# A graph network's attention and three graph convolutions: one-hots made by ScalarE, sort and exponentials through PSUM, and gathered rows moved inside SBUF

## The chip, the cores and the metric

The kernel runs on one core of a Trainium2 chip. A core has five engines that each run their own list of instructions in order: TensorE (PE in the profile, its weight loads PEld), VectorE (DVE), ScalarE (ACT), GpSimd (POOL) and SyncE (SP), which here issues most DMAs. Sixteen DMA engines move data between DRAM (HBM), and the on-chip memory SBUF, which has 128 partitions; TensorE writes its results into PSUM, a second memory of 128 partitions in banks. Engines wait for each other through semaphores. The metric is the device time of one execution in microseconds (us); lower is better. The kernel before takes 6156.63 us, the median of three runs (6151.24 to 6157.75).

## What is computed

A graph of 12500 nodes with 128 features and 200000 edges, sorted by their destination. In short:

```python
h = relu(layernorm(x))
q, k, v = h @ Wq.T, h @ Wk.T, h @ Wv.T                 # 8 heads of 16
scores = einsum(q[dst], k[src]) / 4 + edge_attr @ We.T  # per edge and head
ex = exp(scores - segment_max(scores, dst)[dst])
x = x + segment_sum(v[src] * ex, dst) / segment_sum(ex, dst)
h = relu(layernorm(x))
# three times, with self loops and norm = deg**-.5 at both ends:
#   h = segment_sum((h @ W)[src] * norm, dst) + b ; (relu) ; batch_norm over the nodes
x = x + h
```

All is float32.

## The kernel before

The destination nodes are cut into 106 tiles of 118 (`TN`); a tile's edges lie in a window of 2048 consecutive edges (16 on each of 128 partitions). The program is written in a framework that takes the order of instructions on each engine from priorities and its own plan of the work, and adds all semaphores; each engine then runs its list in that order, and a buffer of a pool is reused when its last reader is done.

**Prologue.** Layer norm, q and the pairs k, v are computed and written to DRAM.

**Attention** (`fast`, from line 885). For each tile GpSimd issues 16 indirect gathers (`gather`, line 148) of 128 rows of k and v into one of three `kv` buffers. VectorE makes `oht` (line 1013), which tells for each edge which of the 128 nodes is its destination, from the edges' node numbers `dw_b`. TensorE multiplies it with q (line 1019), VectorE multiplies the result with k (line 1020) and sums within heads (line 1023). After the edges' bias, scans along the edges give each destination's maximum (lines 1051 to 1075). ScalarE takes the exponential (line 1081), VectorE multiplies it with v (`vals`, line 1082) and makes the second one-hot `oh`, of 16 x 118 columns (line 677), and TensorE sums per node (line 1089).

**Sort.** Between the tiles' instructions, from tile 24 on, `place_edges` prepares the convolutions: a bitonic sort of each tile's edges by source, with all tiles side by side on 106 partitions. Each of its steps is two VectorE instructions of 1024 elements (`swap`, lines 701 and 702). Further steps rank the edges and place each into a slot: for each tile and each of 98 blocks of 128 source nodes there are 13 slots (`SB`), and edges beyond go to an overflow list of at most 768 (`OV`). `go_on` takes the next steps of this at four places of each tile.

**Convolutions** (`conv_slots`). h, scaled, lies in SBUF as `hs` (98 blocks) and in DRAM as `t_d`. The tiles are taken in 12 blocks of nine (9 x 13 = 117 rows). `take` goes through the 98 blocks of sources in seven groups of 14: VectorE turns slot numbers into one-hots `go` (line 1221), TensorE picks the rows (line 1224), ScalarE copies them to `stage` (line 1226), and SP stores `stage` to a table `m` in DRAM (line 1228). `reduce` works one block behind: for each tile six indirect gathers fetch the overflow rows, SP reads the tile's slots from `m` as `mr`, 128 partitions with 10 rows each (line 1245), VectorE makes the one-hot of 16 x 118 from `nums`, a copy of 0 to 117 in PSUM (line 1249), and TensorE sums 10 + 6 products (lines 1253 and 1255) and the tile's own rows (`tg`, line 1159). `finish` does this for three tiles at a time (`GN`), scales, and `use1` to `use3` apply weights, bias and relu. The results h of a convolution stay in SBUF in `big`; only the second half of the first one's 256 features goes to DRAM. When all tiles are done, the batch norm's factors go into the next weights, and `transform` multiplies h by these and writes the next `hs` and `t_d`. If a tile had more overflow than fits, another path (`conv_rows`) would gather each edge's row.

## Time and profile before

| | us |
|---|---|
| median of three runs | 6156.63 |
| the profiled execution | 6154.56 |
| its span | 6152.8 |
| prologue | 0 to 148 |
| attention with the sort | 148 to 2963 |
| the three convolutions | 3008 to 4028, 4091 to 5071, 5113 to 6093 |
| the two transforms, the end | 4034 to 4085, 5076 to 5106, 6097 to 6153 |
| busy: PE, DVE, ACT, POOL | 4406.0, 3396.2, 1011.7, 4084.2 |

The page of a profile gives, for one execution, the busy time of each engine, the span in 40 slices with each engine's busy share in tenths, the DMA engines' share and the TensorE clock that was granted, and then groups of instructions: line, engine, operation, output<-inputs, count, busy time, mean ns of one, and the idle time of the engine just before them with what ended it. Other views show single lines, the instructions in order of time, busy times in chosen stretches, and who waited for whom.

### The profile page before, as it was taken

The numbers are of one execution on the slowest core, as the hardware profiler recorded it, in microseconds if no ns is written. First come the engines' busy times: TensorE is split into PE (matmuls) and PEld (weight loads), VectorE is DVE, ScalarE is ACT, GpSimd is POOL, SyncE is SP. The second block draws the span as 40 slices with busy tenths as digits, with TensorE's granted clock in tenths as the row PEclk, the third lists the DMA queues.
The fourth block names the chain that finished last, engine by engine and source line by source line (L and its number), as shares of the span: only waits on it lengthen the run. The fifth ranks groups of instructions, "written<-read, shape, count | busy, mean of one in ns | idle before, by whom it ended". The sixth has DMA issues, their size and how long they took to land. (4 is left out here: it accounts for less than half of the span.)

```text
span 6152.8 us, 80384 instructions
## 1 busy us (share of the span) xinstructions
PE 4406.0 (72%) x28564; PEld 4115.5 (67%) x28564; DVE 3396.2 (55%) x5972; ACT 1011.7 (16%) x2374; POOL 4084.2 (66%) x3617
## 2 busy tenths in 40 slices
PE   6676666666666665767487787877787787778777
PEld 2666655555566665666377777777777776777777
DVE  7566688887876677655243343353343344434344
ACT  3111111110111111111112122111121211112120
POOL 0777788888888888777266566636666664666663
PEclk9677766666676776767788888898888888888888
DMA  6555544433444444454588888878888887888888
GB/s 188 152 143 138 137 112 106 113 103 109 105 128 120 122 112 112 131 132 114 150 214 216 218 216 218 213 209 217 219 216 221 213 211 204 219 219 219 221 215 209
DMA packets 607714, 1051.07 MB, mean 171 GB/s; under 512 B 191227, under 2 KB 418491, under 8 KB 607201
## 3 DMA queue, kind: packets, MB, share of 16 engines
q1 hardware_dynamic: 464311, 695.85, 41.5%
q0 software_dynamic: 142608, 348.39, 23.9%
q8 instruction: 232, 3.80, 0.3%
q14 instruction: 175, 1.43, 0.1%
q10 hardware_dynamic: 388, 1.60, 0.1%
HBM read 773.19 MB, written 272.26 MB: 170 GB/s over the span
## 5 line engine op out<-in xcount | busy, mean ns | idle before, releaser
L148 POOL DMA_INDIRECT rows<-t_d,srcO x1908 | 1827.6, 958 | 1329.2 <-issue 560.2
L148 POOL DMA_INDIRECT kv<-kv_d,srcA x1696 | 2252.3, 1328 | 536.7 <-issue 484.3
L1249 DVE TENSOR_TENSOR oh<-nums,dlS 128x1888 f32<-128x1888 f32 x318 | 674.3, 2121 | 1527.2 <-PE zp L1255 1517.9
L1253 PE MATMUL zp<-oh,mr 128*128 128x118 f32 x6360 | 966.6, 319 | 567.5 <-DMA mr<-m 440.4
L1253 PEld LDWEIGHTS zp<-oh,mr 128*128 128x128 f32 x6360 | 925.5, 233 | 586.4 <-DMA mr<-m 348.7
L1019 PE MATMUL qe<-qt,oht 128*128 128x128 f32 x3392 | 841.4, 415 | 247.3 <-DVE kv L1020 110.7
L1224 PE MATMUL gp<-hs,go 128*117 128x128 f32 x7056 | 891.8, 281 | 125.8 <-DVE go L1221 69.8
L1019 PEld LDWEIGHTS qe<-qt,oht 128*128 128x128 f32 x3392 | 767.1, 310 | 289.7 <-issue 166.8
L1224 PEld LDWEIGHTS gp<-hs,go 128*117 128x117 f32 x7056 | 831.9, 184 | 165.1 <-issue 117.1
L1226 ACT COPY stage<-gp 117x512 f32<-117x512 f32 x1008 | 521.8, 532 | 1375.0 <-PE gp L1224 936.8
L1020 DVE TENSOR_TENSOR kv<-qe,kv 128x512 f32<-128x512 f32 x424 | 289.4, 685 | 678.8 <-DMA kv<-kv_d,srcA 536.8
L1089 PE MATMUL acc<-vals,oh 128*118 128x137 f32 x3392 | 539.8, 329 | 150.5 <-DVE vals L1082 150.0
L1089 PEld LDWEIGHTS acc<-vals,oh 128*118 128x118 f32 x3392 | 522.1, 225 | 171.6 <-DVE vals L1082 171.3
L1221 DVE TENSOR_SCALAR go<-gi,iota_q 128x468 f32<-128x468 uint8 x1008 | 427.8, 456 | 224.5 <-DMA gi<-gi_d 111.8
L1255 PE MATMUL zp<-oh,rows 128*128 128x118 f32 x3816 | 513.2, 288 | 0.2 <-DMA rows<-t_d,srcO 0.2
L1255 PEld LDWEIGHTS zp<-oh,rows 128*128 128x128 f32 x3816 | 492.2, 206 | 0.4 <-DMA rows<-t_d,srcO 0.4
L1058 PE MATMUL ends<-ident,mg 128*8 128x128 f32 x212 | 53.0, 343 | 344.4 <-DVE mg L1053 305.6
L1082 DVE TENSOR_TENSOR vals<-kv,vals 128x2048 f32<-128x2048 f32 x106 | 242.3, 2286 | 27.2 <-ACT vals L1081 26.8
L1058 PEld LDWEIGHTS ends<-ident,mg 128*8 128x8 f32 x212 | 11.7, 96 | 366.1 <-DVE mg L1053 298.8
L1023 DVE TENSOR_REDUCE sc<-kv 128x128 f32<-128x2048 f32 x106 | 240.8, 2272 | 0.0
L677 DVE TENSOR_TENSOR oh<-iota_f,dlA 128x1888 f32<-128x1888 f32 x106 | 224.0, 2113 | 5.0 <-PE acc L1089 5.0
L1036 PE MATMUL sm<-wbd,et 128*128 128x32 f32 x848 | 167.8, 351 | 45.0 <-DVE mg L1075 37.7
(242 smaller groups left out, 3648.1 us busy)
## 6 DMA issues: line engine op xcount, KB each, us to landing
m<-stage SPq DMA_DIRECT2D x252, 784.0 KB
mr<-m SPq DMA_DIRECT2D x318, 560.0 KB
dw_b<-dlb_d SPq DMA_DIRECT2D x106, 512.0 KB
gi<-gi_d SPq DMA_DIRECT2D x252, 204.8 KB
rows<-t_d,srcO POOLq DMA_INDIRECT x1908
kv<-kv_d,srcA POOLq DMA_INDIRECT x1696
ebx<-in_edge_attr_dram SPq DMA_DIRECT2D x106, 256.0 KB
mr<-m SPq DMA_DIRECT2D x318, 75.0 KB
```

The lines of the kernel that those rows point to most:

```text
L148: nc.gpsimd.indirect_dma_start(out=o, out_offset=None, in_=table[:, :], in_offset=bass.IndirectOffsetOnAxis(ap=idx, axis=0))
L1019: nc.tensor.matmul(qe[:, k, :], ohv[:, :, j + k], qt, start=True, stop=True)
L1020: nc.vector.tensor_tensor(qk[:, j:j + 4, :], qe, qk[:, j:j + 4, :], op=ALU.mult)
L1023: nc.vector.tensor_reduce(sc.rearrange("p h j -> p j h"), qk.rearrange("p j (h c) -> p j h c", h=H), AX.X, ALU.add)
L1082: nc.vector.tensor_tensor(vh[:, :, :, :C], kv[:, :, D:].rearrange("p j (h c) -> p j h c", h=H), vh[:, :, :, C:].to_broadcast([P, JJ, H, C] ...
L1089: nc.tensor.matmul(acc, oh[:, j, :], va[:, j, :], start=(j == 0), stop=(j == JJ - 1))
L1221: nc.vector.tensor_scalar(go[:, :n], gv[:, a:a + n], iota_q, None, op0=ALU.is_equal)
L1224: nc.tensor.matmul(gp[:, i, :], go[:, i].rearrange("p t k -> p (t k)"), hs[:, g * SG + a + i, :], start=True, stop=True)
L1226: nc.scalar.copy(stage[:, a:a + n, :], gp[:, :n, :])
L1249: nc.vector.tensor_tensor(oh, nums.unsqueeze(1).to_broadcast(sh), dlS[:, t, :].unsqueeze(2).to_broadcast(sh), op=ALU.is_equal)
L1253: nc.tensor.matmul(zp[:, i, :], mr[:q, j, :], oh[:q, j, :], start=False, stop=False)
L1255: nc.tensor.matmul(zp[:, i, :], rows[:, j, :], oh[:, RC + j, :], start=False, stop=(j == JO - 1))
```

## The change

In the attention `oht` and `oh` are now made by ScalarE: the absolute value of a difference, then relu(1 - that), which is 1 where the two numbers are equal and 0 elsewhere. The exponentials go to PSUM (`ex`), from which VectorE takes them for `vals` and ScalarE copies them into `vals`' last columns. In the sort each step is cut into two halves, and of each half ScalarE first copies the upper operand to PSUM (`hc`); since there are twice as many pieces, `go_on` takes two at each place. PSUM tiles `nb` and `sm` share buffers, and `acc` has one buffer instead of two.

In the convolutions there are 16 slots instead of 13, an overflow of 512 instead of 768, so four gathers for a tile instead of six, and blocks of eight tiles (14 of them; 8 x 16 = 128 rows). `m` in DRAM is gone: SP moves `stage` from SBUF to SBUF, into `mr`, which holds all eight tiles. Partition q x 16 + s of `mr` holds slot s of a group of 7 (first part) or 6 (second part) sources; the first part has 8 such groups, the second 7. Each transfer fills the 16 partitions of one group from the 128 partitions of `stage`. The sums run in two parts as well: `add_first` adds 7 products for a tile into PSUM while the second part is being taken, `add_rest` adds the own rows, 6 products and the 4 of the overflow while the next block's first part is being taken. Four tiles share a PSUM tile, which a matmul with zeros opens. `big` is gone: all of h goes to DRAM (`h_d`) and is read back by `transform` and by the last stage.

```diff
 WE = 2048
 MG = 4
-SB = 13
-OV = 768
+SB = 16
+OV = 512
 JO = OV // P
 TB = P // SB
-GN = 3
-SG = 14
+CA, CB = 7, 6
 NOT = 1 << 23
...
-    assert TB % GN == 0
-    RC = -(-SL // P)
-    LP, LR = divmod(SL, RC)
-    assert NS % SG == 0 and 112 < LP < P and LR and RC * P <= WE and NS * P * P < LATE and TN < P
+    assert TB * SB == P and TB % NG == 0 and SL <= WE and NS * P * P < LATE and TN < P
+
+    NA = TB * CA
+    NQ = (NS - NA) // CB
+    assert NA + NQ * CB == NS and NQ <= TB
+    parts = [(0, CA, TB), (NA, CB, NQ)]
+    RC = CA + CB
+
+    batches = [[(0, q, 2) for q in range(0, TB, 2)], [(1, q, min(2, NQ - q)) for q in range(0, NQ, 2)]]
+    MB = 2 * CA
     NBK = -(-NTT // TB)
 
...
+        def batch(b, part, q, m):
+            s0, n, _ = parts[part]
+            s0, n = s0 + q * n, n * m
+            return s0, n, gi_d[b, TB * SB * s0:TB * SB * (s0 + n)].rearrange("(t k) -> t k", t=TB)
...
             def swap(lo, hi, lo2, hi2):
-                nc.vector.tensor_tensor(lo2, lo, hi, op=ALU.min)
-                nc.vector.tensor_tensor(hi2, lo, hi, op=ALU.max)
+                n, d = lo.shape[1:]
+                for k in range(2):
+                    cut = (slice(None), slice(k * n // 2, (k + 1) * n // 2)) if n > 1 else (
+                        slice(None), slice(None), slice(k * d // 2, (k + 1) * d // 2))
+                    hc = ps.tile([P, WE // 4], FP, name="hc")[:NTT].rearrange(
+                        "t (n d) -> t n d", n=max(1, n // 2))
+                    nc.scalar.copy(hc, hi[cut])
+                    yield
+                    nc.vector.tensor_tensor(lo2[cut], lo[cut], hc, op=ALU.min)
+                    nc.vector.tensor_tensor(hi2[cut], lo[cut], hc, op=ALU.max)
...
+            niota = once.tile([P, 1], FP, name="niota")
+            nc.vector.tensor_scalar(niota, iota_q, -1.0, None, op0=ALU.mult)
+
+            def where_zero(x):
+
+                nc.scalar.activation(x, x, AF.Relu, bias=ones[:, 0:1], scale=-1.0)
+
...
                     oht = wk.tile([P, WE], FP, name="oht")
-                    nc.vector.tensor_scalar(oht, dw_b, iota_q, None, op0=ALU.is_equal)
+                    nc.scalar.activation(oht, dw_b, AF.Abs, bias=niota[:, 0:1])
+                    where_zero(oht)
...
-                    nc.scalar.activation(vh[:, :, :, C], mx.rearrange("p h j -> p j h"), AF.Exp)
+                    nc.scalar.activation(ex, mx.rearrange("p h j -> p j h"), AF.Exp)
                     nc.vector.tensor_tensor(vh[:, :, :, :C], kv[:, :, D:].rearrange("p j (h c) -> p j h c", h=H),
-                                            vh[:, :, :, C:].to_broadcast([P, JJ, H, C]), op=ALU.mult)
-                    go_on(1)
+                                            ex.unsqueeze(3).to_broadcast([P, JJ, H, C]), op=ALU.mult)
+                    nc.scalar.copy(vh[:, :, :, C], ex)
+                    go_on(2)
                     oh = wk.tile([P, JJ, TN], FP, name="oh")
-                    one_hot(oh, dlA[:, t, :])
-                    acc = ps2.tile([TN, H * (C + 1) + 1], FP, name="acc")
+                    for j in range(JJ):
+                        nc.scalar.activation(oh[:, j, :], iota_f[:, :TN], AF.Abs, bias=dlA[:, t, j:j + 1], scale=-1.0)
+                    where_zero(oh)
+                    acc = ps1.tile([TN, H * (C + 1) + 1], FP, name="acc")
                     for j in range(JJ):
                         nc.tensor.matmul(acc, oh[:, j, :], va[:, j, :], start=(j == 0), stop=(j == JJ - 1))
                     nc.scalar.copy(att[:, i, :], acc)
...
+                def pool(name, bufs, **kw):
+                    return s.enter_context(tc.tile_pool(name=name, bufs=bufs, **kw))
+
+                gy, gx, sg, mt, ga, ohs, wk = (pool(n, b) for n, b in (("gy", 2), ("gx", 3), ("sg", 2), ("mt", 2),
+                                                                         ("ga", 6), ("ohs", 2), ("wk", 2)))
+                pn, pg, pz, ph = (pool(n, b, space=PSUM) for n, b in (("pn", 1), ("pg", 2), ("pz", 3), ("ph", 2)))
+                nums = pn.tile([P, TN], FP, name="nums")
                 nc.vector.tensor_copy(nums, iota_f[:, :TN])
-                blocks = s.enter_context(tc.tile_pool(name="blocks", bufs=3, space=DRAM))
-                gy = s.enter_context(tc.tile_pool(name="gy", bufs=3))
-                gx = s.enter_context(tc.tile_pool(name="gx", bufs=3))
-                sg = s.enter_context(tc.tile_pool(name="sg", bufs=2))
-                mt = s.enter_context(tc.tile_pool(name="mt", bufs=3))
...
+                def ones_at(dl):
+                    oh = ohs.tile([P, CB + JO, TN], FP, name="oh")
+                    sh = [P, dl.shape[1], TN]
+                    nc.vector.tensor_tensor(oh[:, :sh[1]], nums.unsqueeze(1).to_broadcast(sh),
+                                            dl.unsqueeze(2).to_broadcast(sh), op=ALU.is_equal)
+                    return oh
+
+                def take(b, part, mr):
+                    n = parts[part][1]
+                    for _, q, m in batches[part]:
+                        s0, w, slots = batch(b, part, q, m)
+                        gi = gy.tile([P, P * MB], U8, name="gi")
+                        nc.sync.dma_start(gi[:, :P * w], slots.rearrange("t k -> (t k)").unsqueeze(0)
+                                          .to_broadcast([P, P * w]))
+                        gv = gi[:, :P * w].rearrange("p (t s k) -> p s k t", t=TB, k=SB)
+                        stage = sg.tile([P, MB, D], FP, name="stage")
+                        for a, c in groups(w, 4):
+                            go = gx.tile([P, 4, SB, TB], FP, name="go")
+                            nc.vector.tensor_scalar(go[:, :c], gv[:, a:a + c], iota_q, None, op0=ALU.is_equal)
+                            gp = pg.tile([P, 4, D], FP, name="gp")
+                            for i in range(c):
+                                nc.tensor.matmul(gp[:, i, :], go[:, i].rearrange("p k t -> p (k t)"),
+                                                 hs[:, s0 + a + i, :], start=True, stop=True)
+                            nc.scalar.copy(stage[:, a:a + c, :], gp[:, :c, :])
+                        for i in range(m):
+                            nc.sync.dma_start(mr[(q + i) * SB:(q + i + 1) * SB, :, :n, :],
+                                              stage[:, i * n:(i + 1) * n, :])
                         yield
 
-                def reduce(b, m):
-                    for t0 in range(b * TB, min(NTT, (b + 1) * TB), GN):
-                        n = min(GN, NTT - t0)
-                        zp = ps.tile([P, GN, TN], FP, name="zp")
-
-                        def add(i):
-                            t = t0 + i
+                zps = {}
...
+                def add_first(b, mr):
+                    for t in range(b * TB, min(NTT, (b + 1) * TB)):
+                        if t % NG == 0:
+                            zps[t // NG] = pz.tile([P, NG, TN], FP, name="zp")
+                            nc.tensor.matmul(zps[t // NG].rearrange("p a b -> p (a b)"), zero[:, :P], zero,
+                                             start=True, stop=False)
+                        zp = zps[t // NG][:, t % NG, :]
+                        oh = ones_at(dlS[:, t, :CA])
+                        for j in range(CA):
+                            nc.tensor.matmul(zp, mr[:, t % TB, j, :], oh[:, j, :], start=False, stop=False)
+                        yield
+
+                def add_rest(b, mr):
+                    K = NQ * SB
+                    for t0 in range(b * TB, min(NTT, (b + 1) * TB), NG):
+                        n = min(NG, NTT - t0)
+                        tg = own_rows(wk, table, t0, n)
+                        for t in range(t0, t0 + n):
+                            zp = zps[t // NG][:, t % NG, :]
                             rows = ga.tile([P, JO, D], FP, name="rows")
                             for j in range(JO):
                                 gather(rows[:, j, :], table, srcO[:, t, j:j + 1])
+                            oh = ones_at(dlS[:, t, CA:])
+                            nc.tensor.matmul(zp, tg[:, t - t0, :], ident[:TN, :TN], start=False, stop=False)
+                            for j in range(CB):
+                                nc.tensor.matmul(zp, mr[:K, t % TB, j, :], oh[:K, j, :], start=False, stop=False)
                             for j in range(JO):
+                                nc.tensor.matmul(zp, rows[:, j, :], oh[:, CB + j, :], start=False,
+                                                 stop=(j == JO - 1 and t == t0 + n - 1))
+                            yield
+                        finish(wk, t0, n, zps.pop(t0 // NG), use, ph)
+
+                tiles = iter(())
+                for b in range(NBK):
+                    for part in range(2):
+                        mr = mt.tile([P, TB, CA, D], FP, name="mr")
                         done = 0
+                        for g, _ in enumerate(take(b, part, mr)):
+                            while done < g * TB // (len(batches[part]) - 1):
                                 next(tiles, None)
                                 done += 1
+                        for _ in tiles:
+                            pass
+                        tiles = add_rest(b, mr) if part else add_first(b, mr)
+                for _ in tiles:
+                    pass
+
...
+        def result(wk, t0, n, z, func, bias, st, to):
+
+            h = wk.tile([P, NG * TN], FP, name="h")
+            nc.scalar.activation(h[:, :n * TN], z, func, bias=bias)
+            nc.vector.bn_stats(st[:, t0 // NG, :], h[:, :min(n * TN, N - t0 * TN)])
+            nc.sync.dma_start(to[:, t0 * TN:(t0 + n) * TN], h[:, :n * TN])
...
+        def load_h(sr, h, s0, n):
+            hb = sr.tile([P, NG * P], FP, name="hb")
+            nc.sync.dma_start(hb[:, :n * P], h[:, s0 * P:(s0 + n) * P])
+            return hb
+
+        def transform(sr, ps, wa, row, table):
 
             for s0, n in groups(NS, NG):
-                parts = [big[:, s0 * P:(s0 + n) * P]]
-                for h in more:
-                    hb = sr.tile([P, NG * P], FP, name="hb")
-                    nc.sync.dma_start(hb[:, :n * P], h[:, s0 * P:(s0 + n) * P])
-                    parts.append(hb)
+                fs = [load_h(sr, h, s0, n) for h in h_d[:len(wa)]]
                 tp = ps.tile([P, NG, D], FP, name="tp")
                 for i in range(n):
...
```

`go_on(1)` becomes `go_on(2)` in all four places; `big` is replaced by `hb` in the last stage; `own_rows` is the part of `finish` that loads `tg`.

## The prediction

> **What bounds the kernel now.** I read the page first (shares, slices, costliest groups), then the answer for the gathers' line, the timeline of two attention tiles, the busy times by stage, and TensorE's waits in the second convolution.
>
> ```profile
> span 6152.8 us, 80384 instructions
> ...
> POOL 0777788888888888777266566636666664666663
> PEclk9677766666676776767788888898888888888888
> DMA  6555544433444444454588888878888887888888
> ...
> L148 POOL DMA_INDIRECT rows<-t_d,srcO x1908 | 1827.6, 958 | 1329.2 <-issue 560.2
> L148 POOL DMA_INDIRECT kv<-kv_d,srcA x1696 | 2252.3, 1328 | 536.7 <-issue 484.3
> ```
>
> Two halves with two limits. To 2963 us the attention runs: GpSimd at 0.7 to 0.8, DMA half idle. After it DMA is at 0.8 and GpSimd lower. The gathers of both halves, by line (minimum, median, maximum ns):
>
> ```profile
> L148 POOL DMA_INDIRECT rows<-t_d,srcO x1908: 938/944/1194, 2973.1 to 6088.0; - x191
> L148 POOL DMA_INDIRECT kv<-kv_d,srcA x1696: 941/947/6207, 148.2 to 2930.9; - x189
> L1020 DVE TENSOR_TENSOR kv<-qe,kv x424: 625/691/693, 177.5 to 2934.1; 128x512 f32<-128x512 f32 x142
> ```
>
> Both kinds have the same median, but attention's stretch to 6207. Where, the timeline shows (start, duration, engine):
>
> ```profile
> 1498.80 2.11 DVE L677 TENSOR_TENSOR oh<-iota_f,dlA 128x1888 f32<-128x1888 f32 x1
> 1498.87 2.86 POOL L148 DMA_INDIRECT kv<-kv_d,srcA  x1 [0.30 <-DVE A L702]
> ...
> 1502.03 0.95 POOL L148 DMA_INDIRECT kv<-kv_d,srcA  x1 [0.30 <-issue]
> 1502.47 0.33 SPq L1007 DMA_DIRECT2D qt<-q_d  x1
> 1502.48 0.69 DVE L1020 TENSOR_TENSOR kv<-qe,kv 128x512 f32<-128x512 f32 x1 [0.43 <-PE qe L1019]
> ```
>
> A gather that starts under the one-hot takes 2.86 us and ends with it; one beside L1020, which reads PSUM, takes 0.95. The engine is otherwise back to back: 1676 of 1696 gathers follow the previous one by 0.30 us. So attention lasts as long as GpSimd's chain: 1696 x (0.947 + 0.30) = 2115 us unhindered, plus 2252.3 - 1696 x 0.947 = 646 us of stretching.
>
> ```profile
> 3008.00:4028.00 1020.00, 805.78 (x6096) 776.03 (x6096) 402.19 (x543) 211.04 (x406) 586.68 (x614) 0.88 0.81 214
> 4091.00:5071.00 980.00, 770.49 (x5950) 752.13 (x5951) 383.60 (x510) 191.30 (x371) 608.34 (x635) 0.88 0.84 216
> 5113.00:6093.00 980.00, 768.22 (x5952) 750.21 (x5952) 382.77 (x510) 191.25 (x371) 609.17 (x635) 0.88 0.85 217
> ```
>
> The three convolutions (busy PE, weight loads, DVE, ACT, POOL, clock, DMA share, GB/s): DMA 0.81 to 0.85 with PE at 0.79. What PE waits for in the second:
>
> ```profile
> PE zp L1253 <- DMA mr<-m: 157.4, 31, 8.5
> PE zp L1253 <- issue: 29.9, 6, 5.1
> PE gp L1224 <- DVE go L1221: 12.1, 11, 8.5
> ```
>
> So the rows' way through DRAM sets the pace.
>
> [...]
>
> **Part 1, attention.** *Removed stretching.* I laid each long gather against the VectorE instructions running beside it: L1082 (vals) answers for some 183 us, L677 (oh) 158, L1013 (oht) 93, L701 and L702 (sort) 134; together 568 of 646. All four go or get a PSUM input. 78 remain (the ranking steps after the sort).
>
> *Added.* ScalarE per tile: [...] 10.5 us. Before, ScalarE had (85.5 + 195.8 + 86.5)/106 = 3.5. Now 14; during the sort 264 copies of 0.5 in 39 tiles bring 17. GpSimd's pace is 16 x 1.25 = 20 us, so ScalarE fits below it. Table loads keep their number (59 in either order).
>
> VectorE: in the first 602 us it was busy 371 for about 24 tiles, 15 a tile; less 2.1 + 1.3, and less some 1.5 for the loads of edges later, leaves 10.2. Sort halves cost 0.61 each (L1020's spacing) x 528 = 322 over tiles 24 to 63 in the built order: 8.3 a tile, total 19. The ranking, 157 us, now falls into nine tiles instead of 28: 17 a tile, total 27. There VectorE, not GpSimd, is the bound.
>
> *Sum.* 24 tiles x 20.8 = 499; 39 x 22.5 = 878 (VectorE 19, waiting for ScalarE's copies in order; with no waits 20.5, with many 27); 9 x 31 = 279; 34 x 20.4 = 694; tail 35: 2385 against 2815 (148 to 2963). **Gain 430**, from 250 to 550. The chain of one tile after its last gather (about 16 us from the groups' means) has 40 us in three kv buffers. The 112 and more small writes of slot tables (12 before) cost SP 0.35 each, 40 us in all, beside a queue with room; nothing, at most 40.
>
> **Part 2, the convolutions.** *TensorE.* Spacing in the trace is 0.121 for each half of a 128-column matmul, 0.1115 for 118. Slots 13 to 16 make blocks of 8 tiles, not 9: 14 blocks, 98 x 14 x 2 x 0.121 = 332 (285 before). Per tile 7 + 6 + 4 + 1 matmuls instead of 10 + 6 + 1: 106 x 18 x 2 x 0.1115 = 426 (402). So 758 against 687: 71 dearer, 56 a block.
>
> *DMA removed:* write and read of m, 70 + 69 MB per convolution (191 + 252 us of engine time by the packets), a third of the rows' gathers (168 to 112). GpSimd loses 636 gathers and was not the bound. *Added:* 14 x 98 x 64 KB = 90 MB from SBUF to SBUF. Each transfer, 459 or 393 KB, lands on 16 partitions[...]. [...] about 16 (90 MB at 26 GB/s an engine, the trace's best 7168-byte packet at 272 ns). [...]
>
> *A block.* Other traffic per engine: slots' tables 6.4, dinv 3.4, own rows 3.5, gathers 8: 21 us. [...] I take 8 as not hidden, bounds 2 and 21. In the built order each part's first sum stands only 0.2 to 5.3 us of PE work behind its last source, with two stage buffers; PE thus waits for a landing while at most two batches are in flight: 7 us of idle queue a block, bounds 3 and 9. 59 + 8 + 7 = **74 a block** (68 to 80). 14 x 74 + 20 for filling = 1056 against 980: +76, thrice **+228**. The first convolution's 40 extra stay.
>
> *h through DRAM.* The two transforms (51 and 30 us) and the end (56) each read 6.4 MB more at about 237 GB/s, 27 each; some is loaded ahead: **+65** (45 to 80). Stores of h run in the block's spare engine time; the group of four and its zero matmul (27 x 0.2) count nothing.
>
> *Total.* -430 + 228 + 65 = -137: span 6016. The profiled execution took 6154.56, its span 6152.8, the median is 6156.63: forecast 6015 to 6020 for the median, I give 6015.
>
> **Rivals.** [...] (two transfers to neighbouring partitions overlap). Then PE bounds: 56 + 4 of boundary waits, 14 x 60 + 20 = 860, -120 each: -430 - 360 + 65, 5430. [...]
>
> *Slower: [...]* They stand on SP's queue with the tables and own rows[...]: 59 + 16 + 9 = 84 a block, 1196, +216 each, total +283: 6435. It decides from 77.3 us a block on, where three times +122 eats 430 - 65. Near my 74, hence its weight.
>
> *ScalarE becomes attention's bound:* exp and the sort's copies queue behind 6 us of one-hots, tiles stay at 26 us, 50 gained: 6395. Against: 14 to 17 of 20 us.
>
> That the change falls back to the slower row-wise path needs over 512 overflow edges in a tile; the inputs have at most 476.
>
> **Chances.** A run tells about 0.2% from none. Likeliest case 0.42 (68 to 80 a block: 5764 to 6268; faster 0.35, same 0.03, slower 0.04)[...], ScalarE 0.10 (0.03 still faster). Faster 0.62, same 0.03, slower 0.35. The range 5420 to 6450 leaves out the ends of the outer cases.
>
> **What would show it.** kv gathers with a mean near 1.0 us and the last one near 2350 (right), a pace of 26 us a tile with ScalarE full (wrong). In the convolutions: packets of 3584 bytes above 400 ns and PE waiting for mr<-stage[...], or near 150 ns and PE above 0.9 busy[...]. VectorE's instructions of 1.2 us on L723 would show the sort's halves dearer.

## The result, and the profile after

The changed kernel takes 6999.28 us (median of 4 runs, 6996.75 to 7007.39), the kernel before beside it 6157.19: **13.7% slower**, a ratio of 1.1367 with a 95% interval of 1.1347 to 1.1387. The forecast was 6015 us, 5420 to 6450.

The page of the kernel after, in the same parts as shown of before:

```profile
POOL 1767677766866762233323212333323123333230
PEclk8777777777677777888888868787878778878787
DMA  6666555544455647888888858888888888888888
...
L153 POOL DMA_INDIRECT rows<-t_d,srcO x1272 | 1236.6, 972 | 3009.8 <-PE zp L1302 1332.1
L153 POOL DMA_INDIRECT kv<-kv_d,srcA x1696 | 1713.2, 1010 | 747.7 <-issue 466.2
```

In 40 slices of 175 us, attention now ends in the sixteenth, and DMA is at 0.8 to the end. GpSimd's kv gathers took 1713.2 us in place of 2252.3. By line (minimum, median, maximum ns) the median is unchanged; only the long ones are fewer and shorter:

```profile
L153 POOL DMA_INDIRECT kv<-kv_d,srcA x1696: 940/946/4761, 156.2 to 2606.1; - x189
L153 POOL DMA_INDIRECT rows<-t_d,srcO x1272: 938/944/1590, 2650.2 to 6852.5; - x182
```

The busy times by stage of after: first convolution, first transform, second and third convolution (columns as before: PE, weight loads, DVE, ACT, POOL, clock, DMA share, GB/s):

```profile
2685.00:4029.00 1344.00, 905.98 (x6688) 857.65 (x6688) 531.83 (x666) 231.21 (x430) 391.00 (x402) 0.83 0.83 123
4029.00:4162.00 133.00, 80.67 (x400) 73.69 (x401) 38.97 (x76) 1.26 (x4) 0.00 (x0) 0.68 0.48 147
4168.00:5510.00 1342.00, 877.13 (x6584) 850.54 (x6583) 514.82 (x639) 215.70 (x404) 409.20 (x422) 0.81 0.83 119
5571.00:6913.00 1342.00, 877.53 (x6579) 850.99 (x6580) 514.27 (x639) 215.75 (x404) 411.55 (x422) 0.80 0.83 119
```

DMA is as busy as before, 0.83 of the stretch, and moves 119 GB/s in place of 216. Its packets are slow, not many: 79582 in the second convolution where before has 78117, and those of 3584 bytes take 539 ns in the median. The account of the 842 us by which the span grew: the prologue +8, attention -331 (2860 to 2529, from its first gather to the convolutions' first matmul), the convolutions +324, +362 and +363, and +116 (165 to 281) for what lies between and behind them, the two transforms and the end. Who waits in the second convolution (us in total, times, longest):

```profile
DVE go L1266 <- DMA gi<-gi_d: 233.2, 33, 24.7
ACT stage L1271 <- DMA mr<-stage: 231.0, 29, 10.8
...
PE gp L1269 <- DVE go L1266: 141.1, 39, 17.1
...
PE gp L1269 <- ACT stage L1271: 109.1, 38, 8.4
PE zp L1304 <- DMA mr<-stage: 106.4, 7, 15.7
...
PE zp L1288 <- DMA mr<-stage: 54.7, 7, 8.7
```

and SyncE in the same stretch:

```profile
SPq L1273 <- ACT stage L1271: 561.2, 197, 21.2
```

TensorE waits 161 us for landings themselves, but 250 for `go` and `stage`. VectorE's `go` waits for the slots' tables, ScalarE's `stage` for a buffer that is still being copied out. SyncE issues tables and transfers in one order, and stands 561 us at the transfers (L1273) until `stage` is written; what is behind them in its list isn't issued meanwhile.

### The profile page after: what moved, and what is told of

The parts are those of the page before. It is cut to its first block, busy times and chain, and to the rows that moved or that the text cites. A ratio compares the mean times of both kernels' runs of the same rounds, so it can differ in the third digit from the quotient of the medians.

```text
span 6994.6 us, 86241 instructions
## 1 busy us (share of the span) xinstructions
PE 4693.8 (67%) x30420; PEld 4380.2 (63%) x30420; DVE 3477.5 (50%) x6410; ACT 2299.9 (33%) x4848; POOL 2954.0 (42%) x2981
## 5 line engine op out<-in xcount | busy, mean ns | idle before, releaser
L153 POOL DMA_INDIRECT rows<-t_d,srcO x1272 | 1236.6, 972 | 3009.8 <-PE zp L1302 1332.1
L153 POOL DMA_INDIRECT kv<-kv_d,srcA x1696 | 1713.2, 1010 | 747.7 <-issue 466.2
L1269 PE MATMUL gp<-hs,go 128*128 128x128 f32 x8232 | 1230.1, 316 | 771.5 <-DVE go L1266 426.8
L1269 PEld LDWEIGHTS gp<-hs,go 128*128 128x128 f32 x8232 | 1170.3, 226 | 842.9 <-issue 422.8
L1271 ACT COPY stage<-gp 128x512 f32<-128x512 f32 x1134 | 594.6, 547 | 2807.0 <-PE gp L1269 1977.6
L1251 DVE TENSOR_TENSOR oh<-nums,dlS 128x826 f32<-128x826 f32 (+1 forms) x636 | 763.2, 1200 | 1160.4 <-PE zp L1288 877.2
L1266 DVE TENSOR_SCALAR go<-gi,iota_q 128x512 f32<-128x512 uint8 x1134 | 710.2, 656 | 1129.0 <-DMA gi<-gi_d 652.6
L1304 PE MATMUL zp<-oh,mr 112*128 112x118 f32 x3816 | 506.9, 281 | 315.5 <-DMA mr<-stage 315.5
L1304 PEld LDWEIGHTS zp<-oh,mr 112*128 112x128 f32 x3816 | 473.2, 197 | 324.3 <-issue 277.3
L1124 ACT ACTIVATE oh<-iota_f,dlA 128x118 f32<-128x118 f32 x1696 | 512.2, 381 | 0.0
L1118 DVE TENSOR_TENSOR vals<-kv,sm 128x2048 f32<-128x2048 f32 x106 | 241.5, 2278 | 9.7 <-ACT sm L1117 7.7
L1048 ACT ACTIVATE oht<-dw_b,niota 128x2048 f32<-128x2048 bf16 x106 | 211.5, 1995 | 75.7 <-PE qe L1055 70.5
```

What stands on the lines that cost most here:

```text
L153: nc.gpsimd.indirect_dma_start(out=o, out_offset=None, in_=table[:, :], in_offset=bass.IndirectOffsetOnAxis(ap=idx, axis=0))
L1124: nc.scalar.activation(oh[:, j, :], iota_f[:, :TN], AF.Abs, bias=dlA[:, t, j:j + 1], scale=-1.0)
L1251: nc.vector.tensor_tensor(oh[:, :sh[1]], nums.unsqueeze(1).to_broadcast(sh), dl.unsqueeze(2).to_broadcast(sh), op=ALU.is_equal)
L1266: nc.vector.tensor_scalar(go[:, :c], gv[:, a:a + c], iota_q, None, op0=ALU.is_equal)
L1269: nc.tensor.matmul(gp[:, i, :], go[:, i].rearrange("p k t -> p (k t)"), hs[:, s0 + a + i, :], start=True, stop=True)
L1271: nc.scalar.copy(stage[:, a:a + c, :], gp[:, :c, :])
```

## The experiments

**Theory 1**: each transfer of stage into mr lands on 16 neighbouring partitions, and landing there binds: a packet of 3584 bytes takes 539 ns in the median. **Theory 2**: the order of work with two stage buffers binds; TensorE waits for landings whatever their rate. **Theory 3**: copies inside SBUF are slow wherever they land. For attention, whose gain was 100 us short: ScalarE's hand-overs, or the gathers.

The experiments ran in six groups, each beside the kernel before on the same chip. On the three chips of the first five groups the kernel before took 7284 to 7385 us in the median; on that of the last group 6148, like the first comparison. Times are thus compared within a group; stages are compared within chips of one kind, where the kernel before still differs by 100 us. Attention is counted from its first gather (e_kvdirect: its first load of `kv`) to the first matmul of the convolutions, a convolution as the mean of the second and third.

| kernel | us | ratio to before, 95% | attention | convolution |
|---|---|---|---|---|
| *chips like the first* | | | | |
| before | 6157 | | 2860 | 980 |
| after | 6999 | 1.137 (1.135 to 1.139) | 2529 | 1343 |
| e_all | 6014 | 0.978 (0.977 to 0.980) | 2519 | 1045 |
| *the other chips* | | | | |
| c_before | 7410 | one run | 3076 | 1344 |
| c_after | 8829 | 1.195 (1.191 to 1.198) | 3659 | 1576 |
| e_att, e_att2 | 7939, 7827 | 1.077, 1.075 (1.071 to 1.082) | 3608, 3535 | 1347, 1314 |
| e_conv | 8220 | 1.118 (1.112 to 1.124) | 3031 | 1575 |
| e_spread | 8164 | 1.108 (1.103 to 1.112) | 3652 | 1358 |
| e_stages | 8514 | 1.156 (1.149 to 1.163) | 3652 | 1509 |
| e_best | 7967 | 1.092 (1.089 to 1.095) | 3602 | 1339 |
| e_actq | 8544 | 1.173 (1.168 to 1.177) | 3600 | 1505 |
| e_nogather | 7966 | one run | 3651 | 1291 |
| e_nogather_spread | 7292 | one run | 3653 | 1063 |
| e_hots | 7464 | 1.024 (1.020 to 1.029) | 3190 | 1322 |
| e_psum | 7611 | 1.034 (1.028 to 1.039) | 3272 | 1340 |
| e_mix | 7510 | 1.017 (1.013 to 1.020) | 3284 | 1276 |
| e_kvdirect | 6740 | one run | 2388 | 1343 |
| e_pause | 7942 | 1.078 (1.074 to 1.082) | 3595 | 1345 |
| e_final | 7241 | 0.984 (0.981 to 0.987) | 3035 | 1273 |

### The two halves alone, and controls

e_att and e_att2 are the kernel before with the attention part of the change only; e_conv has all the rest of it; c_after and c_before are the two kernels unchanged.

> The kernel before with only the attention part of the change; convolutions, slots of 13 and h on the chip as before. If the two parts are independent, as the stage times of the two traces say (attention 2815 to 2484 us), the time is 6157 - 331 = 5826 us, convolutions 1020, 980, 980. If the convolutions' loss came from something that the attention part leaves behind, they grow too and the time stays above 6157. The forecast's own term (gain of 430) would give 5727.

> The kernel before with only the second part: slots of 16 in two parts of sources, rows from SBUF to SBUF, h through DRAM; attention as before. Independent parts: 6157 + 1048 (convolutions) + 129 (transforms and end) = 7334 us, each convolution about 1343, attention 2815. The forecast's terms (+228 and +65) would give 6450.

> The attention part alone once more, the same kernel as e_att. On that run's chip the kernel before took 7377 us instead of 6157, with stretches in which SyncE's register instructions took 0.70 us each, and attention grew from 3031 (e_conv, attention as before) to 3608 us. Theory: the gain belongs to a chip that issues instructions at the usual rate: where the kernel before takes about 6157, this takes about 5826 (attention near 2500, convolutions 1020, 980, 980). Rival: the attention part is slower wherever the convolution part is missing (order of instructions, placement): ratio again above 1.05.

> The changed kernel itself, as a control beside the experiments. On the two chips of the experiments the kernel before takes 7280 to 7380 us instead of 6157 and its convolutions some 1330 instead of 980, so the parts have to be compared there: the sum of what e_att2 (+545) and e_conv (+843) added gives about 8670 us where before takes 7280, a ratio of 1.19; if the parts hide one another, as in the first comparison where the gain of one was taken from the loss of the other, 1.14 as there. On a chip like the first one: 6999.

> The kernel before itself, for its trace on the chip of these runs. Theory: while GpSimd issues gathers back to back, signals between the other engines come late on these chips (SyncE's register instructions took over 500 ns in 46 of 100 cases in e_att2 after 12 us of gathers without a break, in none on the first chip); then attention takes about 3030 us as in e_conv and the convolutions 1310 to 1340 with DMA no busier than 820 us of 980. Rival: the chip's DMA is slower; then the 4096-byte packets, 244 ns in the median before, are longer by the same third.

The halves are nearly independent: on those chips they add 543 to 562 and 843 us, together some 1400, and the whole change 1444. The second half costs less there than the 1177 us expected from the first comparison. The sign of the first half was not as expected: it loses 543 to 562 us there, where attention had gained 331. By c_before's trace this is not slower DMA: in the second convolution its packets of 4096 bytes take 229 ns in the median, in the first trace 243, and the DMA engines are busy 800 us in place of 823. The rival of e_att2, that attention is slower wherever the convolution part is missing, falls with c_after, which has both parts and takes 3659 as well. What it is comes further down.

### Where the transfers land

e_spread renumbers mr's partitions, slot by slot, and the one-hots with them; every engine gets the same instructions in the same order.

```
-  ...rearrange("t (c q k) -> t c q k", c=n, k=SB)
+  ...rearrange("t (c k q) -> t c q k", c=n, k=SB)
-  nc.sync.dma_start(mr[(q + i) * SB:(q + i + 1) * SB, :, :n, :], stage[...])
+  at = mr[:parts[part][2] * SB].rearrange("(k q) t c d -> q k t c d", k=SB)[q + i]
+  nc.sync.dma_start(at[:, :, :n, :], stage[...])
```

> The changed kernel with the partitions of mr renumbered, slot-major: a source chunk's 16 slots land on every 8th partition (part 0) or every 7th (part 1) instead of 16 consecutive ones. Same bytes, same transfers, same order of instructions on every engine; only which partitions each transfer reaches. Theory 1 [...] packets of 3584 bytes fall from 539 to below 300 ns, of 3072 bytes below 200, TensorE becomes the bound, a block takes 60 to 70 us, each convolution 860 to 1000 instead of 1342, the kernel 5550 to 5950. Theory 2 (order of work and two stage buffers) and theory 3 (SBUF-to-SBUF traffic is slow wherever it lands): packets and convolutions stay as they are, 1300 to 1342, kernel about 6900 to 7000.

The packets of the second convolution, by the trace's DMA records (median ns; 14336 of 3584 bytes, 12544 of 3072):

| | 3584 bytes, part 0 | 3072 bytes, part 1 | both, of 16 engines' time |
|---|---|---|---|
| after | 539 | 454 | 764 us |
| c_after | 541 | 462 | 772 us |
| e_spread | 268 | 182 | 369 us |
| e_all | 288 | 199 | 400 us |

On neighbouring partitions 16 packets at once make 16 x 3584 / 539 ns = 106 GB/s and 16 x 3072 / 454 = 108. With part 0 on every eighth partition (e_spread), the packets take half as long, 268 ns, or 214 GB/s. Part 1, on every seventh, takes 182 ns and reaches 270. These rates are estimates from the medians for 16 packets in flight (in after 15.5 in the mean where it has eight or more; in e_spread not counted). Theory 1 is shown for the rate; theory 3 falls. How the landing slows the packets was not shown. The second convolution of c_after and of e_spread:

```profile
5537.00:7114.00 1577.00, 959.61 (x6583) 909.05 (x6584) 514.02 (x639) 215.90 (x404) 401.93 (x423) 0.77 0.69 101
```

```profile
5314.00:6675.00 1361.00, 932.02 (x6584) 884.63 (x6584) 513.52 (x639) 216.56 (x404) 401.97 (x423) 0.82 0.49 117
```

DMA falls from 0.69 to 0.49 of the stretch, and 216 us go, nearly all of the 232 by which c_after's convolutions exceed c_before's. The 860 to 1000 that I expected were not reached: the kernel before itself takes 1344 on these chips, and what holds it there comes further down. On a chip like the first, where the change costs some 360 us a convolution, this edit alone was not run.

### Buffers and queue

e_stages: four stage buffers, six in the pool `sr` of the transforms and the end. e_best: e_spread with the six. e_actq: the transfers on ScalarE's queue.

```
-  ("sg", 2), ("mt", 2)                       # e_stages
+  ("sg", 4), ("mt", 2)
-  sr = s.enter_context(tc.tile_pool(name="sr", bufs=3))
+  sr = s.enter_context(tc.tile_pool(name="sr", bufs=6))
-  nc.sync.dma_start(mr[(q + i) * SB:...      # e_actq
+  nc.scalar.dma_start(mr[(q + i) * SB:...
```

> The changed kernel with four stage buffers instead of two in the convolutions, and six buffers instead of three in the transforms and the end. Theory 1[...]: ScalarE and TensorE run further ahead but the transfers are no faster, convolutions 1270 to 1342. Theory 2 (two stage buffers, TensorE waits for the landing): most of the excess goes, convolutions below 1120. First transform: if its 133 us come from both loads of h sharing three buffers, it falls to about 85; if from DRAM bandwidth, it stays above 115.

> The changed kernel with the partitions of mr renumbered as in e_spread and with six buffers in the transforms and the end as in e_stages. In e_spread the packets of 3584 bytes fell from 539 to 268 ns and of 3072 bytes from 454 to 182, but the convolutions, 1361 us, were no faster than those of the kernel before on that chip (1342). [...] on a chip where the kernel before takes about 6157 a convolution takes 860 to 1000 us (TensorE some 60 to 70 a block), attention 2529 with its hand-over, transforms and end 76 + 53 + 74, the kernel 5600 to 6000. If what held e_spread (order, two stage buffers) holds here too, convolutions stay above 1150 and the kernel above 6350.

> The changed kernel with the transfers of stage into mr issued by ScalarE on its own queue instead of SyncE's; partitions as in the change. They no longer stand ahead of the slots' tables, own rows and h on SyncE's queue. [...] a convolution stays at 1250 to 1342 us. If most of the loss is what waits behind them on the queue (tables late, one-hots late, TensorE idle), it falls to [...] 900 to 1050. ScalarE itself pays for 630 issues, estimated from SyncE's 0.37 us each: 80 us a convolution of an engine that is a fifth busy.

More stage buffers save 67 us of c_after's 1576, another queue 71: on these chips theory 2 and the queue are real and small beside the landing. The first case expected of e_best was that the landing alone had bound; its convolutions stayed above 1150 (1339), as the second case had it. In the transforms, from the end of the first convolution to the second, c_after takes 140 us with three buffers for each of `og` and the loads of h, which come two a step there, and e_stages 76 with six (62 to 53 and 80 to 74 in the other two places).

### Gathers and landing, crossed

```
-  for j in range(JO):
-      gather(rows[:, j, :], table, srcO[:, t, j:j + 1])
```

> The changed kernel without the overflow rows' gathers in the convolutions: their matmuls read one zeroed tile, so the rows of edges beyond the slots are left out of the sums. [...] a convolution stays within 59 to 80 us a block: 850 to 1130 us, and packets of 3584 bytes above 450 ns. If the loss in the convolutions is the gathers' (late signals and packets that share the engines), convolutions fall to TensorE's own 860 to 920 with packets as they are.

> The same without the overflow rows' gathers, with the partitions of mr spread as in e_spread (packets of 3584 bytes near 270 ns, of 3072 near 185). Nothing but TensorE and the hand-overs are left: 840 to 920 us a convolution. If it stays above 1100, the order of work and the two stage buffers bind[...]. [...]

| convolution, us | with gathers | without |
|---|---|---|
| 16 neighbouring partitions | 1576 | 1291 |
| spread | 1358 | 1063 |

Landing on neighbouring partitions costs 218 to 228, the overflow rows' gathers 285 to 295, and the two add. Only the first is a loss by the change: the kernel before has these gathers too, six a tile where the change has four. 1291 is above the 850 to 1130 expected if the landing alone bound, and 1063 above TensorE's 854 busy us; TensorE still waits 104 us there for `go`, 45 for landings and 34 for `stage`.

### Attention on the other chips

What differs there: signals come late while GpSimd issues gathers. Timeline of e_att in a convolution, code that the attention part doesn't touch (start, duration, engine, line):

```profile
5564.88 1.20 PE L1242 MATMUL gp<-hs,go 128*117 128x128 f32 x4 [2.87 <-issue]
5565.91 0.94 POOL L148 DMA_INDIRECT rows<-t_d,srcO  x1 [0.30 <-issue]
5569.22 0.86 ACT L1244 COPY stage<-gp 117x512 f32<-117x512 f32 x2 [4.39 <-remote]
5569.22 0.84 DVE L1239 TENSOR_SCALAR go<-gi,iota_q 128x468 f32<-128x468 uint8 x2 [4.51 <-remote]
```

TensorE is done at 5566.08; two engines that wait for it start together 3.1 us later, when the last gather too has ended (5566.85). Likewise SyncE's instructions that only handle registers: they take over 500 ns in 63 of 121 cases that come after 12 us of gathers without a break in c_after, in 13 of 510 outside gathers, and in none of 1062 in the first trace. So on these chips the chain of a tile is slow while GpSimd issues gathers, and GpSimd then waits for its kv buffers. The page's line of c_before and of c_after:

```profile
L148 POOL DMA_INDIRECT kv<-kv_d,srcA x1696 | 2204.2, 1300 | 800.2 <-issue 489.1
```

```profile
L153 POOL DMA_INDIRECT kv<-kv_d,srcA x1696 | 1683.0, 992 | 1894.0 <-DVE vals L1118 1074.1
```

The change removes 521 us of stretching and gets 1094 of waiting, most of it for L1118.

e_hots is the kernel before with the one-hots by ScalarE alone; e_psum keeps them on VectorE, one against numbers in PSUM, with the exponentials through PSUM; e_mix joins it to the repaired convolutions.

```
-  one_hot(oh, dlA[:, t, :])                  # e_psum
+  nc.vector.tensor_tensor(oh, nums.unsqueeze(1).to_broadcast(sh), dlA..., op=ALU.is_equal)
   # nums: 0 to 117 in PSUM
```

> The kernel before with only the one-hots of the attention by ScalarE; exponentials and the sort's halves stay where they were. By the forecast's terms 158 + 93 us of the gathers' stretching go (of 646) and with them 251 us: about 5905 where before takes 6157; gathers' busy time about 2000 us (2252 before, 1713 after). If ScalarE's 10 us a tile cost something themselves (waits for oht or oh), less: above 6000.

> The kernel before with the two attention edits that cost ScalarE nearly nothing: exponentials through PSUM (as in the change), and the one-hot of destinations still by VectorE in one instruction, but against numbers 0 to 117 that lie in PSUM instead of SBUF. No one-hots by ScalarE, no halves of the sort. In the first comparison's trace the two instructions held GpSimd for 183 + 158 = 341 us: where before takes 6157 this takes about 5820. On chips like those of the last runs (before 7280 to 7410, attention 3076): if GpSimd's stretching is still what is paid there, attention falls by a third to all of 341 us; if what binds there is the chain of one tile under late signals, it stays at 3000 to 3100, but does not grow to 3190 (one-hots by ScalarE) or 3600 (whole attention part), since no hand-over is added but one copy.

> The attention of e_psum with the changed convolutions in which mr's partitions are spread (as e_spread), with four stage buffers and six buffers in the transforms and the end (as e_stages). Convolutions: e_best had 1344 with two stage buffers; in e_stages four of them saved 67[...]. If TensorE's wait for the landing is what is left (two stage buffers), they fall to 1150 to 1280 on chips like the last ones, 860 to 950 on one like the first; if late signals under GpSimd's gathers are left, they stay at 1280 to 1344. Kernel: before's 7385, plus 3 times (convolution - 1338), plus 40 for the transforms, plus e_psum's difference: about 7250 on such chips, 5500 to 5650 on one like the first.

e_hots and e_psum missed: both were to gain on a chip like the first, and e_psum at worst to stay on these. e_psum's attention grew by 196 us to 3272 with no new hand-over but one copy, while its gathers fell from 2204.2 to 1894.9 busy us and their waits for `vals` grew from 239 to 681. That fits the view that gathers which follow each other more densely delay the chain, but doesn't show it: e_psum also has the change's single `acc` buffer, and its order of work is planned anew. e_hots loses 180 us (7464 against 7284 on its chip), the whole attention part (e_att2, same chip) 543. e_mix's convolutions, 1276 against e_best's 1339, lie where its two ranges meet and decide nothing.

e_kvdirect replaces a tile's gathers by one plain load of as many bytes; e_pause adds work to GpSimd.

```
-  gather(kv[:, j, :], kv_d, srcA[:, t, j:j + 1])                    # e_kvdirect
+  nc.sync.dma_start(kv, kv_d[:WE].rearrange("(p j) d -> p j d", j=JJ))
+  for _ in range(4 if j % 4 == 3 else 0):                           # e_pause
+      nc.gpsimd.iota(idle, pattern=[[1, 512]], base=0, channel_multiplier=0, ...)
```

> The attention part alone (e_att), with the 16 gathers of a tile replaced by one plain load of as many bytes from fixed rows of the same table on SyncE's queue: the neighbours' own keys and values are left out, every other instruction stays. Theory: with GpSimd out of the way, signals between the engines are on time, and attention runs at the pace of VectorE and ScalarE, 15 to 20 us a tile (1600 to 2150 us) instead of 34 (3608). Rival: VectorE and ScalarE with their hand-overs themselves need some 30 us a tile on such a chip: then attention stays above 3000. SyncE's register instructions over 500 ns (150 of 1276 in e_att) nearly vanish by the theory, and stay by the rival.

> The attention part alone (e_att), with four instructions on GpSimd that write unused numbers to a private tile of 512 columns after every fourth gather: nothing else changes, GpSimd only gets work, some 4 x 4 x 0.5 = 8 us a tile on top of 16 x 1.25 = 20. Theory (signals between the other engines come late while gathers follow each other without a break): in each pause they are delivered, VectorE's chain goes on, and attention gets faster with more work on GpSimd: about 28 to 31 us a tile instead of 34, attention 3000 to 3300 instead of 3530 to 3608. Rival (what counts is the share of time with gathers, or any work of GpSimd): the work comes on top, 34 to 42 us a tile, attention 3600 to 4400.

Without gathers attention takes 2388 us in place of 3608, between the two ranges expected, and SyncE's instructions over 500 ns (reads of a register from memory included) fall from 157 to 19. The other engines alone thus need 22.5 us a tile on such a chip, and GpSimd's gathers alone 20 (16 x 1.25); that both together take 34 means that gathers hold up the chain. Whether by their density, e_pause doesn't settle: its 3595 miss the theory's 3000 to 3300. Its groups on GpSimd:

```profile
L148 POOL DMA_INDIRECT kv<-kv_d,srcA x1696 | 1666.9, 983 | 784.5 <-issue 433.3 <-DVE vals L1101 322.0 <-DMA kv<-kv_d,srcA 15.2
L1027 POOL IOTA idle<- 128x512 f32 x1696 | 971.0, 573 | 84.1
```

The planner set one such instruction after each gather. In tiles 0 to 24, with 0.57 us of added work per gather, the pace went from 34.1 to 27.3 us a tile: faster by more work, as the theory says. In the sort's tiles it stayed (35.6 against 35.4 in tiles 40 to 59), and in tiles 87 to 104 it went from 30.4 to 34.9: no gain in all. What makes these chips differ from the first is open; no run changed it.

### The repair

e_final: the attention of before with the changed convolutions, spread, with four and six buffers. e_all: the same repairs with the change's own attention.

> The attention of the kernel before with the changed convolutions, mr's partitions spread, four stage buffers, six buffers in the transforms and the end. From stage times of runs on the last chip: attention 3076 (c_before), convolutions 1314, 1275, 1277 (e_mix), transforms and end 77 + 54 + 74, against 1328, 1339, 1349 and 65 + 43 + 57 in the kernel before: 7385 - 150 + 40 = 7275 us, a ratio of 0.985. On a chip like the first one, where signals are on time, convolutions of 860 to 950: about 5960 where before takes 6157. If the parts of attention and convolution hide one another, no gain: 7385.

> The whole change with the repairs: mr's partitions spread, four stage buffers, six buffers in the transforms and the end, and the change's own attention. On chips like the last ones: attention 3659 (c_after), convolutions 1289, 1265, 1281, transforms and end 77 + 54 + 75 (e_final): 7860 us where before takes 7370, a ratio of 1.067 against the change's 1.195; two thirds of its loss are then the convolutions'. On a chip like the first one, with attention 2529 to the first convolution and convolutions of 860 to 950: 5450 to 5750 where before takes 6157. If the repairs work only beside the other attention, above 1.15.

e_final takes 1.6% less than before (1.3 to 1.9) on one of the chips with late signals, as worked out from its parts. e_all ran on a chip like the first: 6014 us, 2.2% below before and 14% below the change. Its first transform, second and third convolution:

```profile
3719.00:3795.00 76.00, 54.66 (x404) 49.42 (x405) 43.09 (x82) 1.26 (x4) 1.72 (x2) 0.93 0.81 257
3795.00:4830.00 1035.00, 837.91 (x6583) 814.83 (x6583) 512.15 (x639) 218.09 (x404) 408.05 (x423) 0.91 0.67 155
4883.00:5937.00 1054.00, 838.06 (x6583) 815.03 (x6583) 511.58 (x639) 218.06 (x404) 406.59 (x423) 0.91 0.67 152
```

and TensorE's waits in its second convolution:

```profile
PE gp L1269 <- DVE go L1266: 83.8, 44, 11.0
PE zp L1288 <- DMA mr<-stage: 51.2, 9, 7.8
PE zp L1304 <- DMA mr<-stage: 28.5, 5, 6.0
```

Waits for stage are gone (109.1 to 5.7), those for landings halved. With packets half as long a convolution takes 1045, not the 860 to 950 expected: TensorE is busy 838, and `go` still waits 96 us for its tables. How the 298 us saved divide between landing and buffers on this chip was not measured. A convolution is still dearer than before's 980; what makes e_all faster than before is attention. Attention's half alone was not run on such a chip; by its stages it would take 6157 - 331 = 5826, an estimate.

## Why the prediction was wrong

**The block's time, T = 74, is the step that failed.** It was 59 for mr's packets + 8 for other traffic + 7 idle, and the 59 an assumption that no line of before's trace showed; measured in the same way, with 20 us of a convolution for filling, it is (1342 - 20) / 14 = 94, that is 54.6 + 24.6 + 15.2. The first term held: mr's packets took 764 us of 16 engines in 14 blocks. The second failed: of 21 us of other traffic I took 8 as not hidden, an estimate that no trace showed. For 57% of the second convolution at least eight of mr's packets were in flight, and then 15.5 in the mean, on 16 engines; the gathers' packets of 4096 bytes that began then took 546 ns in the mean, those that began with none in flight 263. Almost nothing was hidden: 59 + 21 would have been 80, and all packets together took 1109 / 14 = 79.2. The third term was too small: 1342 - 1109 = 233 us without work for the DMA engines, 213 without the filling. Tables, own rows and stores of h stand behind the transfers in SyncE's list, `go` comes late, and TensorE's next sources with it; how much of the 233 that is was tried on another chip alone, where another queue for the transfers won 71. Three times +350 is +1049 for +228.

**The slower rival was right on the overlap and too small**: mr's transfers without overlap with the other traffic, 84 a block, at a chance of 0.24. It counted 16 of the other traffic and 9 idle. The decision lay at 77.3 a block, 17 below what came. I had put the likeliest case on the favourable side of an overlap that no line of the trace showed.

**That transfers to neighbouring partitions overlap**, the first rival, also at 0.24, with packets near 150 ns, is refused by 539 ns a packet, and the third rival, ScalarE as attention's bound, too: ScalarE is busy 1587 of attention's 2484 us, and the tiles take 21.7 to 22.6 us before the ranking, not 26.

**Attention**: mechanism right, size 331 for 430. Stretching fell from 646 to 107 (1713.2 - 1696 x 0.947), 539 of the 568: with the one-hots off VectorE and one input of the other three in PSUM, the mean gather fell from 1328 to 1010 ns. By the timelines, gathers that began beside `vals` took 2.57 us in the mean before (L1082, both inputs in SBUF, 93 gathers) and 0.95 after (L1118, one input in PSUM, 145 gathers). ScalarE's instructions had their price (oht 1995 ns each, oh 381). The 10.5 us a tile that I had added for ScalarE were an estimate that before's trace didn't show; in after's the lines L1048, L946, L1124 and L1120 are busy 1172 us, 11.1 a tile, of them 6.7 for `oh`. What was missing in the sum is GpSimd's waiting: 147.2 us for kv buffers until L1118 and 57.1 at one place, where I had counted three buffers as enough. By tiles: 21.7 for 20.8 at the start, 22.6 for 22.5 in the sort, 35.5 in tiles 59 to 62, where the sort ends and I had 22.5; 27.1 for 31 after it, 22.2 for 20.4 at the end. The one place is tile 62:

```profile
1599.87 0.19 PE L781 MATMUL acc<-ones,sm 106*1 106x1 f32 x2 [41.35 <-DVE ci L795]
1610.80 1.80 POOL L153 DMA_INDIRECT kv<-kv_d,srcA  x1 [57.08 <-DVE ci L795]
```

The ranking's check for too much overflow is a small matmul (L781), for which the change takes a buffer of `acc`. TensorE, which works in order, stood at it until VectorE had done the last steps of the sort and the sums behind them; no tile was finished meanwhile, and no kv buffer came free. In the kernel before, TensorE stood 4.6 us at that matmul. Whether the shared buffer or the place in the order does it, no run separates. Of the signs that I had named, the gathers' mean (1010 ns) came out as for the likeliest case; the last gather came at 2606 us, not near 2350. All this is of the first chip; on the others the part loses.

**h through DRAM**: +116 for +65 (139 + 61 + 81 against 63 + 42 + 60). I sized it by bandwidth; the loads of a step take from three buffers, in the first transform two loads a step, and with six the three places cost +36 (76 + 52 + 73).

One reading was off without bearing on T: the packets that write and read m took 218 + 264 us of 16 engines in the second convolution, where I had 191 + 252.

## What to carry to other kernels

Count the partitions on which one transfer lands before counting its bytes: here 16 neighbouring ones took 106 GB/s, every eighth 214. Then add all other traffic of the engines to the packets' time: here it wasn't hidden, 79.2 us a block for all packets where 59 + 8 had been counted. Renumbering the slots so that the rows of one transfer land eight partitions apart halved the time of its packets (541 to 268 ns, c_after to e_spread), with the same instructions. A gain in one stage is to be measured on more than one chip: the attention part gained 331 us on one and lost 543 to 562 on others. When a tile moves to DRAM, the pool that it is loaded into needs its depth set anew (the first transform took 140 us with three buffers in c_after and 76 with six in e_stages), and when a small instruction borrows a buffer, look at what then stands behind it (TensorE stood 41.35 us at L781).

## What the runs showed of the hardware

- Copies from SBUF to SBUF, by their packets' median (after and e_spread, estimated for 16 packets at once): 106 to 108 GB/s onto 16 neighbouring partitions, 214 onto every eighth, 270 onto every seventh.
- Other packets are slowed beside transfers that land on 16 neighbouring partitions: in after's second convolution the gathers' packets of 4096 bytes took 546 ns in the mean where eight or more of mr's were in flight as they began, and 263 where none was; in e_all, with the landing spread, 302 and 317.
- On the three chips of the first five groups, and not on those of the first comparison and of e_all, signals came late under gathers: SyncE's register instructions took over 500 ns in 63 of 121 cases in c_after and in none of 1062 in the first trace. There the change's attention part lost 543 to 562 us where it had gained 331, and the kernel before took 7284 to 7385 us in place of 6157. The granted clock was lower too (0.748 in c_before, 0.796 in the first trace); which of these is cause and which effect is open.
